# Token loads of the QKV stages: the group behind the next one loaded at a group's 30th product

## The chip, the cores and the metric

The kernel runs on one NeuronCore of one Trainium2 chip. The metric is the time of one execution on the device in microseconds (us); lower is better. Five engines work side by side, each through its own instructions in order: PE (TensorE, matrix products and transposes), DVE (VectorE), ACT (ScalarE), POOL (GpSimd) and SP (SyncE, which here only issues DMAs).

## The reference

One transformer block with adaptive layer norm, for 2 batches of 2048 tokens with 512 features, all in float32: 

```
mod = silu(condition) @ Wada + bada            # six vectors per batch
xm  = layernorm(x, g1, be1) * (1 + sc_a) + sh_a
qkv = xm @ Wqkv                                # 16 heads of 32
x   = x + gt_a * (causal_attention(q, k, v) @ Wproj + bproj)
xm  = layernorm(x, g2, be2) * (1 + sc_m) + sh_m
x   = x + gt_m * (gelu(xm @ W1 + b1) @ W2 + b2)    # 2048 hidden
```

## The kernel before

The two batches are taken one after the other: QKV stage, attention, then the output projection, and at the end the two MLP products for both batches. The projection of batch 0 is interleaved with the preparation of batch 1's QKV stage.

**The QKV stage** (`class Qkv`, `run`). The 2048 tokens are four groups of 512 (`NG` = 4, `MT` = 512). A group's products follow a Strassen-like scheme with seven products in place of eight: token operands are halves of the transposed, normalized tokens `xmT` and differences of these (`token_sum`, tiles `t`), weight operands are blocks of Wqkv and their sums. For each of four chunks of 128 features of q and k (`keys_and_queries`) and then twice for v (`values`) there are seven steps of two 128x256 products by halves; in the trace they are `ps_a`, `ps_b` and `ps_c`. A group so has 42 steps (`STEPS`), and behind each step stands a call of `tick`, which does the side work due at that step number `n`. The seventh step of a chunk is put off behind the first two steps of the next one. With it q or k is split into a high and a low part (`hi`, `lo`; ACT casts, DVE or POOL subtracts) and both are stored to scratch in DRAM through SP (L1031).

**What `tick` does for the next group g + 1.** At n = 3 `load_x(g + 1)` issues four DMAs on SP (L919), one for each 128 tokens, into the four buffers of tile `x`. At n = 10 to 13 DVE takes the statistics of each (`stat`, L218; after the last `rstd` and `shift`, L224 to L226). At n = 15 and 25 ACT scales the tokens in place, two tiles each (L964). At n = 18 and 28 PE transposes them (`ps_xt`, L214) and ACT applies the modulation into `xmT`. At n = 36 to 40 follow the token differences. Group 0 of batch 0 is loaded at the start; for batch 1 groups 0 and 1 are loaded in the projection phase before.

Because there are four buffers of `x` and a group has four tiles, a load must wait until the transposes that read the former group from them are done.

**Other side work in the same ticks.** From group 1 on the first attention scores are already computed between the steps: PE writes a score bank `s` (two banks, pool `ps_s`) and DVE reduces it to row maxima (`mx`; L504 for whole rows, L498 for the causal block). PE cannot write a third score before DVE has reduced the first. In batch 0 the modulation products `ps_mod` take a bank of the same pool, which DVE frees with the sum `mr` (L1425). `Pieces` (its `load` and `add`) loads blocks of W1 (batch 0) and of W2 (batch 1) on SP at fixed tick counts (L1230, L1239), lets POOL form weight sums of them (L1251), and stores these to DRAM for the MLP. The loads fill buffers that are free at that time, named `kst`, `qst` and `vv` in the trace. From n = 10 a group's keys and queries are read back in the layout of the attention (L335, L360).

**What sets the order.** A planner of the tile framework gives each engine one fixed list of instructions. PE's products and many others are kept in the order of the program; the rest is placed by the planner's estimate of when its inputs are ready. SP works through its list in order, and an issue that waits for a buffer, or for data of another engine, holds all issues behind it. SP's list follows the program here.

Of the kernel before, what the change touches and what calls it, by code (L numbers as in the profile page):

```python
# [27 lines left out]
def dit_block_kernel(  # L28
# [46 lines left out]
    NG = T // MT  # L75
# [132 lines left out]
    def act(ins):  # L208

        return tc.keep_in_program_order(ins)  # L210
# [687 lines left out]
    class Qkv:  # L898
# [239 lines left out]
        def run(self, hp, also, early=()):  # L1138

            row = self.row  # L1140
            late = []
            for g in range(NG):
                at = [0]

                def tick():
                    n, at[0] = at[0], at[0] + 1
                    if n >= self.STEPS:
                        return
                    if g + 1 < NG:
                        if n == 3 and g + 1 not in self.xts:  # L1150
                            self.load_x(g + 1)
                        if 10 <= n < 10 + MTT and g + 1 > row.b:
                            self.stats(g + 1, n - 10)
                        if n in (15, 25):
                            self.scaled(g + 1, n // 25)
                        if n in (18, 28):
                            self.norm(g + 1, n // 28)()
                        sums = {36: S1, 38: S2, 40: S3}
                        if n in sums:
                            self.token_sum(g + 1, sums[n])  # L1160
                    elif n == 28:

                        row.rows(0)
                        act(nc.scalar.activation(first, eps, AF.Exp))
                    if g > 0 and n == 2:
                        self.token_sum(g, A22)
                    if n > 9 and self.loads:
                        self.loads.pop(0)()
                    also(g, n)
                    if g > 0 and n >= 7:  # L1170


                        past, of = n - 6, self.STEPS - 7
                        if g == 1:
                            row.score(row.count(cum[0] * past / of, 0))
                        else:
                            past += of * (g - 2)
                            row.score(
                                row.count(
                                    cum[0] + (cum[2] - cum[0]) * past / (2 * of),  # L1180
                                    1 if g == 2 and n < 25 else 2,
                                )
                            )

                for u in range(C + 2):
                    if (g, u) in early:
                        for k, step in enumerate(self.plain(g, u, hp)):
                            step()
                            if k:
                                tick()  # L1190
                        self.token_sum(g, S3)
                        continue
                    if u < C:
                        steps = self.keys_and_queries(g, u, hp)
                    else:
                        steps = self.values(g, u - C)
                    for step in steps[:2] + late + steps[2:6]:
                        step()
                        tick()
                    late = steps[6:]  # L1200
            for step in late:
                step()
            assert not self.loads
# [156 lines left out]
    with pool("wada") as wp, pool("qkv0") as qp, pool("hl0") as hp, pool(  # L1360
# [113 lines left out]
        def also(g, n):  # L1474

            if (g, n) == (0, 7):
                for k in range(4):
                    qkv.weight_sum(nc.gpsimd, k, slice(0, P))
            pieces.tick()
            if g == 0 and n == 22:  # L1480
                load_wada(2, 5)
            elif g in (1, 2) and n == 10:
                qkv.columns = modulation(g + 1)
            elif g in (1, 2) and n == 14:
                qkv.columns()
                if g == 1:
                    load_wada(3, 4)
                else:
                    scale_shift(a2, c2, r_g2, r_be2, 3, 4)
# [837 lines left out]
```

## Time and profile before

| | us |
|---|---|
| median of 3 runs | 2256.44 (2254.54 to 2258.32) |
| profiled execution | 2256.73 |
| its span in the profile | 2255.0 |
| QKV stage of batch 0, groups 0 to 3 | about 28 to 64, 64 to 106, 106 to 155, 155 to 208 |
| QKV stage of batch 1, groups 0 to 3 | about 777 to 816, 816 to 858, 858 to 906, 906 to 956 |

A row of the timeline gives the start in us, the length in us, the engine, the line, the operation, what it writes and reads, and the count of equal instructions merged in it. In brackets stands the time for which the engine was idle before it, and whose end released it. `SPq` is the issue of a DMA, not its transfer. A row of the waits gives the waiting engine and tile, what it waited for, the sum in us, the count and the longest. The granted clock is the share of full speed at which PE was allowed to run.

### The profile page before, as it was taken

To read this page: it belongs to the slowest core of one execution; us is meant where nothing else is said; L and a number is where in the kernel's file an instruction comes from. 1 tells how busy PE (TensorE), PEld (TensorE's weight loads), DVE (VectorE), ACT (ScalarE), POOL (GpSimd) and SP (SyncE) were. 2 spreads that over 40 slices of the span, in tenths; PEclk is the share of its full clock that TensorE was granted. 3 is DMA by queue.
4 is the path that set the end of the run, shared out by engine and by line. 5 is a ranking of instruction groups with operands and counts; after the bars stand their busy time and mean duration, and the time that the engine had idled before them with its cause. 6 is when DMAs were issued, how large, how long until landed. Compare 5 with 4: busy or idle time off the path is not lost.

```text
span 2255.0 us, 33464 instructions
## 1 busy us (share of the span) xinstructions
PE 2211.3 (98%) x12057; PEld 1432.2 (64%) x12057; DVE 1535.7 (68%) x3309; ACT 1004.6 (45%) x2012; POOL 1297.9 (58%) x807
## 2 busy tenths in 40 slices
PE   7999999999999999999999999999999999999998
PEld 6777555555543587855555555345787787688687
DVE  4668766777757666777577767663685586576576
ACT  4434555555564244365656555614322422332410
POOL 4253998998983695199989898444205204304210
PEclk9999999999999999999999999999999999999999
DMA  8877143231324799542324113363353354353433
GB/s 281 251 259 193 43 93 75 62 85 48 106 97 135 252 308 313 142 92 62 85 67 104 44 48 131 109 231 129 109 175 133 123 184 145 108 187 126 158 125 110
DMA packets 160510, 311.57 MB, mean 138 GB/s; under 512 B 16544, under 2 KB 48844, under 8 KB 158552
## 3 DMA queue, kind: packets, MB, share of 16 engines
q1 hardware_dynamic: 155488, 285.53, 41.8%
q0 software_dynamic: 4480, 23.36, 2.7%
q8 instruction: 95, 1.56, 0.3%
q14 instruction: 71, 0.58, 0.1%
q10 hardware_dynamic: 376, 0.55, 0.1%
HBM read 229.95 MB, written 87.29 MB: 141 GB/s over the span
## 4 chain that ended last, share of the span: by engine, by line
PE 89%; DVE 4%; DMA 2%; POOL 2%; ACT 1%; issue 1%; SPq 0%; DVEq 0%; ACTq 0%; POOLq 0%
PE ps_a L206 27%; PE st L206 18%; PE ps_b L206 12%; PE o L206 10%; PE s L206 9%; PE ps_c L206 4%; PE ps_o L206 4%; PE sm L206 3%; DVE junk L498 1%; POOL ee L695 1%; PE ps_xt L214 1%; DMA x<-in_x_dram 1%; ACT e L670 1%; DVE mx L504 1%; PE ps_o L214 1%
## 5 line engine op out<-in xcount | busy, mean ns | idle before, releaser
L670 ACT ACTIVATE e<-st 128x512 f32<-128x512 f32 (+1 forms) x1152 | 575.0, 579 | 362.4 <-PE st L206 321.3
L504 DVE TENSOR_REDUCE mx<-s 128x1 f32<-128x512 f32 x576 | 381.9, 686 | 199.0 <-PE s L206 197.9
L695 POOL TENSOR_TENSOR ee<-ee,e 128x2048 f32<-128x2048 f32 x106 | 485.8, 4583 | 10.3 <-ACT e L670 4.3
L206 PE MATMUL st<-qst,kst 128*128 128x512 f32 (+3 forms) x1280 | 408.7, 386 | 0.0
L206 PE MATMUL s<-kst,qst 128*128 128x512 f32 (+3 forms) x1046 | 382.2, 396 | 8.0 <-DVE mx L498 2.7
L206 PE MATMUL ps_a<-sum,w 128*128 128x256 f32 (+1 forms) x1088 | 328.8, 431 | 0.1
L206 PE MATMUL o<-e,vv 128*32 128x512 f32 (+3 forms) x2560 | 293.2, 537 | 0.3 <-POOL e L682 0.3
L206 PEld LDWEIGHTS st<-qst,kst 128*128 128x128 f32 x1280 | 228.5, 188 | 97.3 <-issue 65.7
L498 DVE CUSTOM_DVE_ANT_0 junk<-s,causal 128x128 bf16<-128x128 f32 (+3 forms) x470 | 220.7, 470 | 61.0 <-PE s L206 46.8
L1795 POOL TENSOR_TENSOR sum<-w 128x256 f32<-128x256 f32 x30 | 21.8, 727 | 397.1 <-DMA w<-w1d 203.1
L206 PEld LDWEIGHTS s<-kst,qst 128*128 128x128 f32 x1046 | 195.4, 189 | 72.4 <-DVE mx L504 15.4
L206 PEld LDWEIGHTS ps_a<-sum,w 128*128 128x128 f32 x1088 | 204.5, 190 | 40.1 <-issue 11.4
L695 POOL TENSOR_TENSOR ee<-e 128x2048 f32<-128x2048 f32 x42 | 192.5, 4583 | 43.5 <-ACT e L670 42.5
L206 PEld LDWEIGHTS <-sel 32*128 32x128 bf16 x1152 | 29.5, 91 | 197.0 <-issue 196.1
L2014 ACT ACTIVATE h<-h,cols 128x512 f32<-128x512 f32 x120 | 76.8, 710 | 136.3 <-DVE h L1716 136.3
L504 DVE TENSOR_REDUCE mx<-st 128x1 f32<-128x512 f32 x192 | 131.0, 682 | 0.5
L682 POOL TENSOR_SCALAR_AFFINE_SELECT e<-e 128x512 f32<-128x512 f32 x128 | 83.3, 669 | 67.2 <-ACT e L670 67.2
L206 PE MATMUL st<-fold,sel 32*128 32x512 bf16 (+1 forms) x1152 | 117.3, 372 | 1.2
L206 PEld LDWEIGHTS o<-e,vv 128*32 128x32 f32 x2560 | 59.1, 108 | 92.3 <-issue 72.8
L1716 DVE TENSOR_TENSOR h<-c,ps_b 128x256 f32<-128x256 f32 x90 | 37.9, 421 | 103.5 <-PE ps_b L206 103.0
L1066 POOL TENSOR_TENSOR lo<-lo,hi 128x512 fp32r<-128x512 f32 x32 | 40.7, 1274 | 114.2 <-ACT hi L1064 109.8
L206 PE MATMUL ps_b<-sum,w 128*128 128x256 f32 (+1 forms) x384 | 95.0, 383 | 0.0
(237 smaller groups left out, 3590.7 us busy)
## 6 DMA issues: line engine op xcount, KB each, us to landing
qst<-q SPq DMA_DIRECT2D x128, 256.0 KB
kst<-k SPq DMA_DIRECT2D x128, 256.0 KB
w<-w1d SPq DMA_DIRECT2D x32, 896.0 KB
w<-w2d SPq DMA_DIRECT2D x28, 1024.0 KB
w<-w2d SPq DMA_DIRECT2D x28, 768.0 KB
q<-hi SPq DMA_DIRECT2D x32, 256.0 KB
q<-lo SPq DMA_DIRECT2D x32, 256.0 KB
k<-hi SPq DMA_DIRECT2D x32, 256.0 KB
```

The lines of the kernel that those rows point to most:

```text
L206: return tc.keep_in_program_order(nc.tensor.matmul(*args, **kw))
L214: return tc.keep_in_program_order(nc.tensor.transpose(dst, src, ident[:n, :n]))
L498: nc.vector.tensor_tensor_reduce(junk[:, :w], x, causal[:, QB - w :], 1.0, MASKED, ALU.add, ALU.max, m,)
L504: self.vector(nc.vector.tensor_reduce(m, x, axis=AX.X, op=ALU.max))
L670: act(nc.scalar.activation(e4[:, h, :w], sts[h][:, :w], AF.Exp))
L682: nc.gpsimd.affine_select(d, d, pattern=[[0, HC], [1, P]], compare_op=ALU.is_ge, fill=0.0, base=0, channel_multiplier=-1,)
L695: act(nc.gpsimd.tensor_tensor(dst, x, y, ALU.add))
L1066: engine.tensor_tensor(lo, d, hi.bitcast(F32), ALU.subtract)
L1716: act(nc.vector.tensor_tensor(dst, x, y, ALU.add))
L1795: act(engine.tensor_tensor(dst, u, v, op))
L2014: nc.scalar.activation(d[j], d[j], AF.Gelu, bias=col(r_b1 + half * HF + fs[j], 1))
```

## The change

In `tick` of a group g a second place for the load is added: at n = 30, two steps behind the last transposes of group g + 1, the tokens of group g + 2 are loaded, if there is such a group. At n = 3 of the next group the load is left out when it has been made (the old condition `g + 1 not in self.xts` does that). This concerns groups 2 and 3 of each batch; group 1 of batch 0 is still loaded at n = 3 of group 0. The order of PE's instructions is the same in both builds. SP's list differs for group 3 of each batch, and DVE's, ACT's and POOL's lists near it in some places, since the planner puts the statistics, the scaling, a cast and a subtraction where it now expects their inputs.

```
                     n, at[0] = at[0], at[0] + 1
                     if n >= self.STEPS:
                         return
+                    if n == 30 and g + 2 < NG:
+                        self.load_x(g + 2)
                     if g + 1 < NG:
                         if n == 3 and g + 1 not in self.xts:
                             self.load_x(g + 1)
                         if 10 <= n < 10 + MTT and g + 1 > row.b:
                             self.stats(g + 1, n - 10)
```

Lines behind the insertion move by two: L1230 of before is L1232 of after, L1251 is L1253.

SP's list near group 3, before and after:

```
batch 0, before:  k store (hi, lo)  kst<-W1 x4  x x4  q store (hi, lo)
batch 0, after:   k store (hi, lo)  x x4  kst<-W1 x4  q store (hi, lo)
batch 1, before:  k store (hi, lo)  vv/kst<-W2 x8  x x4  q store (hi, lo)
batch 1, after:   k store (hi, lo)  x x4  vv/kst<-W2 x8  q store (hi, lo)
```

More of the change, by code (lines that the diff above doesn't have):

```diff
@@ L1148, in tick @@
                         return
+                    if n == 30 and g + 2 < NG:
+                        self.load_x(g + 2)
                     if g + 1 < NG:
```

## The prediction

> **What bounds the kernel now.** I read the page's busy shares and the chain first, then the waits of TensorE (PE) in the eight group windows of the two QKV stages, then the granted clock there, and last the queues of SP, DVE and PE at each token load.
>
> ```profile
> span 2255.0 us, 33464 instructions
> PE 2211.3 (98%) x12057; PEld 1432.2 (64%) x12057; DVE 1535.7 (68%) x3309; ACT 1004.6 (45%) x2012; POOL 1297.9 (58%) x807
> PE 89%; DVE 4%; DMA 2%; POOL 2%; ACT 1%; issue 1%; SPq 0%; DVEq 0%; ACTq 0%; POOLq 0%
> PE ps_xt L214 <- ACT x L964: 1.4, 2, 1.0
> PE s L206 <- DVE mx L498: 2.7, 1, 2.7
> PE ps_xt L214 <- ACT x L964: 1.4, 2, 1.0
> PE ps_xt L214 <- ACT x L964: 4.2, 2, 3.8
> ```
>
> PE is busy 98% of the span and holds 89% of the chain, so time is won only where PE idles or runs at a low clock. The four waits are of the windows 64 to 106, 106 to 155, 816 to 858 and 858 to 906 us: groups 1 and 2 of batch 0, then of batch 1. In each, the tokens of the following group come late: 1.4, 2.7, 1.4 and 4.2 us. Two of them also cost clock:
>
> ```profile
> 74.00:78.00 4.00, 3.07 (x15) 2.40 (x14) 3.67 (x14) 2.64 (x7) 0.00 (x0) 1.00 0.78 225
> 120.00:121.00 1.00, 1.00 (x3) 0.82 (x4) 1.00 (x3) 0.00 (x0) 0.00 (x0) 0.50 1.03 325
> 125.00:126.00 1.00, 1.00 (x4) 0.76 (x4) 0.72 (x3) 0.00 (x0) 0.92 (x2) 0.53 0.36 131
> 877.00:878.00 1.00, 0.62 (x4) 0.62 (x4) 0.00 (x0) 1.00 (x2) 1.00 (x1) 0.50 1.02 166
> 880.00:881.00 1.00, 1.00 (x5) 0.82 (x5) 0.41 (x2) 0.95 (x2) 1.00 (x3) 0.86 1.10 229
> ```
>
> The columns are window and length, busy time of PE, weight load, DVE, ACT and POOL, then the granted clock, DMA share and GB/s. After the 2.7 us gap the clock is 0.50 for six windows of 1 us (first and last shown); after the 3.8 us gap for three, and 0.86 in a fourth. Around the gap of 1.4 us it is 1.00.
>
> **The change, part by part.** It adds and removes no instruction on a computing engine; it moves DMA issues. Four loads could move: group 2 and group 3 of each batch.
>
> *Group 2, both batches: nothing.* In the old order the load stands at the third product of group 1, in the new at the 30th of group 0. Between these places no piece of W1 or W2 is loaded in either batch (pieces are loaded at ticks 26 and 58 of batch 0, 16 and 47 of batch 1; the interval is ticks 30 to 45). SP, which takes its issues in order, has the same order in both builds: the load stands right behind the k store of chunk 3.
>
> ```profile
> 58.57 0.34 SPq L1031 DMA_DIRECT2D k<-lo  x1
> 59.00 1.83 SPq L919 DMA_DIRECT2D x<-in_x_dram  x4
> 816.80 0.32 SPq L1031 DMA_DIRECT2D k<-lo  x1
> 817.21 1.83 SPq L919 DMA_DIRECT2D x<-in_x_dram  x4
> ```
>
> So the two 1.4 us waits stay. The change does in two places of four what its name says.
>
> *Group 3, batch 0: about 5.7 us won.*
>
> ```profile
> 88.92 0.87 PE ps_xt L214 x8
> 107.57 4.91 SPq L1230 DMA_DIRECT2D kst<-in_L_cond_W_dram  x4
> 112.58 1.84 SPq L919 DMA_DIRECT2D x<-in_x_dram  x4
> 110.72 2.02 DVE L504 TENSOR_REDUCE mx<-s 128x1 f32<-128x512 f32 x3 [0.62 <-PE s L206]
> 115.91 0.69 DVE L218 BATCH_NORM_STATS2 stat<-x 128x6 f32<-128x512 f32 x1 [2.07 <-DMA x<-in_x_dram]
> 118.51 0.69 DVE L218 BATCH_NORM_STATS2 stat<-x 128x6 f32<-128x512 f32 x1 [0.90 <-DMA x<-in_x_dram]
> 119.12 0.67 DVE L498 CUSTOM_DVE_ANT_0 junk<-s,causal 128x512 bf16<-128x512 f32 x1
> 113.90 1.92 PE L206 MATMUL ps_mod<-vv,sc 128*32 128x512 f32 x16
> 116.09 1.02 PE L206 MATMUL ps_b<-xmT,wqk 128*128 128x256 f32 x4
> 119.86 0.80 PE L206 MATMUL s<-kst,qst 128*128 128x512 f32 x1 [2.75 <-DVE mx L498]
> 123.55 1.27 POOL L1066 TENSOR_TENSOR lo<-lo,hi 128x512 fp32r<-128x512 f32 x1 [6.78 <-ACT hi L1064]
> 106.00:155.00 49.00, 45.24 (x214) 37.27 (x215) 33.26 (x89) 19.05 (x42) 18.52 (x20) 0.93 0.86 272
> ```
>
> The four x issues move ahead of four piece issues that take 4.91 us, so they start at about 107.6 instead of 112.6. The transposes that read the buffers ended at 89.8, so their wait is over by then. The first tile landed 3.3 us after its issue (112.58 to 115.91) and the third 5.9 us after: now about 110.9 and 113.5. DVE's new order takes the first statistic after two of the three reductions, at 112.0, and the rest after the fourth (it ends at 113.8). None waits for x any longer. The adaptive-norm sum reads `ps_mod`, which ends at 115.8, and L498 reads the score after it: it ends near 117.2, and PE is ready for its next score at 117.1. The 2.75 us gap shrinks to about 0.1. Without it the half clock goes too: six windows at half speed are 3.0 us. That makes 2.75 + 3.0 - 0.1, about 5.7 us, and at most 5.85. What could be late next are the scaled tokens at the transposes; among PE's waits of this window none is for them, and `shift` in the new order follows reductions that PE itself paces, so it moves forward with PE. The lower end is 0, for a load that lands no earlier.
>
> The four piece loads come at least 1.84 us later (the four x issues). They feed sums of POOL, whose results the MLP stage reads over a thousand us later. The cover is POOL's idle time, 6.8 us ahead of its next `lo`; without it a late `lo` would hold the k and q stores. I cost it at nothing.
>
> *Group 3, batch 1: about 3.8 us won.*
>
> ```profile
> 861.25 0.93 SPq L1239 DMA_DIRECT2D vv<-in_L_cond_W_dram  x2
> 865.36 1.84 SPq L919 DMA_DIRECT2D x<-in_x_dram  x4
> 865.31 0.42 DVE L1072 SCALAR_TENSOR_TENSOR lo<-ps_b,lo 128x256 f32<-128x256 f32 x1 [0.22 <-issue]
> 869.84 0.69 DVE L218 BATCH_NORM_STATS2 stat<-x 128x6 f32<-128x512 f32 x1 [0.36 <-DMA x<-in_x_dram]
> 874.98 0.80 DVE L226 SCALAR_TENSOR_TENSOR shift<-mv,rstd 128x4 f32<-128x4 f32 x1
> 871.87 1.03 PE L206 MATMUL ps_b<-xmT,wqk 128*128 128x256 f32 x4
> 876.68 0.33 PE L214 MATMUL ps_xt<-ident,x 128*128 128x128 f32 x1 [3.79 <-ACT x L964]
> 877.38 1.75 PE L214 MATMUL ps_xt<-ident,x 128*128 128x128 f32 x7 [0.38 <-ACT x L964]
> 879.36 1.49 PE L206 MATMUL ps_c<-xmT,wqk 128*128 128x256 f32 x4
> 869.33 1.28 POOL L1251 TENSOR_TENSOR vv<-vv,kst 128x512 f32<-128x512 f32 x1 [0.55 <-DMA kst<-in_L_cond_W_dram]
> 887.73 3.73 POOL L1066 TENSOR_TENSOR lo<-lo,hi 128x512 fp32r<-128x512 f32 x3
> 897.73 0.62 ACT L1064 CAST hi<-lo 128x512 fp32r<-128x512 f32 x1 [2.00 <-DMA q<-hi]
> ```
>
> Here x passes eight piece issues, 861.25 against 865.36, 4.1 us. But DVE is the limit: from 865.3 to 875.8 it runs with idle times of 0.2 to 0.4 us (two of them in the rows). The new order puts the statistics between the score reductions, and two reductions and an L1072 behind `shift`; at about 0.6, 0.6 and 0.4 us each that is 1.6 us, so `shift` ends near 874.2 by counting, and near 873.3 if the waits in between go too. Against that, the statistics hold back two reductions that free score banks: I place waits of PE of 1.2 and 0.6 us at the scores near 868 and 870. PE then reaches the transposes at 874.7 instead of 872.9, and the scaled tokens are there (first transpose 0.9 us after `shift` ends, as before: 876.68 less 875.78). From there to the end of `ps_c` it took 4.2 us (876.68 to 880.85) and should take 2.1 at full clock. So `ps_c` ends at 876.8: about 4.0 us won, 3.8 with another small wait. Upper end: all of the two gaps (4.2) and the clock, 5.7 (0.62 us busy at half speed, two windows whole, one at 0.86: 0.3 + 1.0 + 0.1, about 1.5). Lower end: 0, where the inserted statistics cost PE what the early tokens give; a loss is excluded by nothing but the count above, and belongs to the last rival.
>
> POOL's sums of the delayed pieces start near 871.2 instead of 869.33, and one `lo` now stands in their midst, so the two others, part of the three at 887.73, end about 2 us later than before. The cast that reuses the first one's `hi` buffer comes at 897.7 in the old trace, 893.7 with PE 4 us earlier, and POOL's `lo` ends at 892.1: 1.6 us of cover. Beyond it PE would lose one for one.
>
> *Sum.* 5.7 + 3.8 = 9.5 us. The profiled execution took 2256.73 (span 2255.0), the median of the runs is 2256.44: 2247.2 and 2246.9. I say 2247. The chain through the attention phases behind both stages is PE's own work, so I expect the gain to last.
>
> **Rivals.**
> 1. *The clock falls in batch 1 all the same.* The 3.8 us gap splits into waits of 1.2, 0.6 and perhaps 0.5 us within 6 us. For: a gap of 2.75 us was enough at 119.9. Against: 1.4 us in the window 74 to 78 left it at 1.00, and the batch 1 gaps lie apart with products between. It would cost up to six windows at half speed, 3.0 us: 2250. [...]
> 2. *DVE takes batch 1 back.* The statistics displace reductions one for one. For: DVE is full there. Against: the counted 1.6 us. Only batch 0 gains: 2256.4 - 5.7 = 2250.7.
> 3. *The loads land no earlier.* The DMA share is 0.86 in the window 106 to 155 (row above); the store of a W1 sum and the token load may share the same engines, so that an early issue only queues longer. Against: 3.3 us and 4.5 us from issue to first statistic under the same load. Then the old waits return: 2256.
> 4. *Slower: the statistics block DVE.* They now stand ahead of score reductions, and PE has two score banks. If x lands later than DVE reaches it, DVE waits, the reductions behind it wait, and PE stops. In batch 0 this breaks even when the first tile lands at 115.9, 8.3 us after the issue, and each further us costs PE one. To lose over 4.5 us in all, the tiles of both batches would have to land some 10.6 us after issue: 2261 or more. Nearest rows: 3.3 and 4.5 us.
>
> **How the numbers follow.** A measurement here tells about 0.2%, 4.5 us, from no change. Forecast 0.54 (2247), rival 1 0.17 (2250), rival 2 0.15 (2250.7), rival 3 0.09 (2256), rival 4 0.05 (2261). The range goes from 2244 (both upper ends, 5.85 + 5.7, give 2244.9, and the runs scatter by 2) to 2252 (rival 2 with a scatter of 1) and leaves out rivals 3 and 4, 0.14. Faster is forecast and rivals 1 and 2, 0.86, less 0.04 because rival 2 lies near the 2251.9 bound: 0.82. Same 0.12, slower 0.06.
>
> **What would show it.** Right: SP issues the tokens of group 3 directly behind the k store, near 107.6 and, 5.7 us earlier, near 855.6, with the piece loads behind; no wait of a statistic for x; PE clock 1.00 from 117 to 126; the waits of 1.4 us for group 2 unchanged; the transposes in batch 1 begin about 7.7 us earlier than at 876.68, 5.7 of them batch 0's. Wrong: a DVE statistic waiting for x ahead of a reduction; new waits of PE `s` for DVE `mx` over 2 us in all; a clock of 0.50 near 870; ACT casts waiting for POOL `lo` near 890.

## The result, and the profile after

| | runs | median us | ratio to the kernel before, 95% interval |
|---|---|---|---|
| before | 22 | 2258.05 | 1 |
| changed kernel | 22 | 2252.53 | 0.9974 [0.9968, 0.998] |
| changed kernel, measured again with e9 and e10 | 7 | 2250.54 | 0.9967 [0.9955, 0.9979] |
| changed kernel, measured again with e12 | 8 | 2250.47 | 0.9976 [0.9965, 0.9986] |

The change makes the kernel 0.26% faster, 5.9 us by this ratio (the two medians differ by 5.5). The forecast was 9.5 us and a time of 2247 (2244 to 2252): the direction was right, but only about three fifths of the gain came. The profiled execution took 2252.46 us, span 2250.7.

First the lines that answer to the prediction's first fence, from the page of the changed kernel and from the waits of PE in the windows 64 to 106, 106 to 155, 810 to 852 and 852 to 902 us:

```profile
span 2250.7 us, 33467 instructions
PE 2210.1 (98%) x12057; PEld 1429.4 (64%) x12057; DVE 1537.3 (68%) x3309; ACT 1003.6 (45%) x2012; POOL 1298.3 (58%) x807
PE ps_xt L214 <- ACT x L964: 1.4, 2, 1.0
PE ps_mod L206 <- DVE mx L504: 0.9, 1, 0.9
PE ps_xt L214 <- ACT x L964: 0.9, 2, 0.6
PE s L206 <- DVE mx L504: 0.9, 2, 0.7
PE ps_b L206 <- ACT vv L1130: 0.4, 1, 0.4
```

The waits for group 2 (first and third of them) are still there, as forecast. The two waits for group 3 are gone: 2.7 us in batch 0 has become 0.9 on another bank of the same pool, and 4.2 us in batch 1 has become 0.9 at the scores, 0.3 at the transposes and a new 0.4 on a copy into `vv`. The granted clock around both old gaps, in windows of the changed kernel (columns as in the prediction):

```profile
118.00:130.00 12.00, 11.96 (x66) 9.14 (x59) 10.99 (x27) 5.56 (x12) 6.18 (x8) 1.00 0.93 272
870.00:890.00 20.00, 19.47 (x100) 16.90 (x100) 14.60 (x42) 10.83 (x24) 19.71 (x25) 1.00 0.95 284
```

It is full in both. The same windows of the kernel before had 0.72 (row under e1 and e2 below) and 0.91:

```profile
870.00:890.00 20.00, 15.84 (x73) 13.51 (x72) 13.37 (x39) 9.24 (x19) 19.70 (x25) 0.91 0.95 295
```

So most of the waits and all of the half clock went. To see why less came of it than forecast, I compare the start of the same PE instruction in each profile with its start in the first profile of the kernel before (PE's order is equal in all of them), and take the difference over a stretch. Negative is time won.

| profile | batch 0, 108 to 127 us | batch 1, 866 to 882 us | behind it, 893 to 905 us |
|---|---|---|---|
| before | 0 | 0 | 0 |
| before, second profile (e5) | -2.8 | +1.7 | 0.0 |
| batch 1 alone (e2); batch 0 is old code | -1.9 | -4.3 | +1.1 |
| batch 0 alone (e1); batch 1 is old code | -4.3 | -0.3 | 0.0 |
| changed kernel | -4.6 | -3.9 | +0.6 |
| changed kernel (e11, e13) | -4.2, -4.0 | -4.2, -4.5 | +0.7, +1.3 |
| load one product earlier (e7, e12) | -5.9, -5.9 | -5.2, -5.2 | +1.9, +0.5 |

Two things stand out. The old code of batch 0 is itself 1.9 and 2.8 us faster in other profiles than in the one the forecast was made from. And behind batch 1 something is given back that no profile of the old code shows. The experiments go after both.

### The profile page after: what moved, and what is told of

The parts are those of the page before. It is cut to its first block, busy times and chain, and to the rows that moved or that the text cites. A ratio compares the mean times of both kernels' runs of the same rounds, so it can differ in the third digit from the quotient of the medians.

```text
span 2250.7 us, 33467 instructions
## 1 busy us (share of the span) xinstructions
PE 2210.1 (98%) x12057; PEld 1429.4 (64%) x12057; DVE 1537.3 (68%) x3309; ACT 1003.6 (45%) x2012; POOL 1298.3 (58%) x807
## 4 chain that ended last, share of the span: by engine, by line
PE 88%; DVE 4%; POOL 3%; DMA 2%; ACT 1%; issue 1%; SPq 0%; DVEq 0%; ACTq 0%; POOLq 0%
PE ps_a L206 26%; PE st L206 18%; PE ps_b L206 12%; PE o L206 10%; PE s L206 9%; PE ps_c L206 4%; PE sm L206 3%; PE ps_o L206 3%; DVE junk L498 1%; POOL ee L695 1%; PE ps_xt L214 1%; ACT e L670 1%; DVE mx L504 1%; PE ps_o L214 1%; DVE stat L218 1%
## 5 line engine op out<-in xcount | busy, mean ns | idle before, releaser
L504 DVE TENSOR_REDUCE mx<-s 128x1 f32<-128x512 f32 x576 | 381.6, 686 | 193.4 <-PE s L206 192.4
L504 DVE TENSOR_REDUCE mx<-st 128x1 f32<-128x512 f32 x192 | 131.0, 683 | 0.6
L1066 POOL TENSOR_TENSOR lo<-lo,hi 128x512 fp32r<-128x512 f32 x32 | 40.6, 1274 | 103.9 <-ACT hi L1064 102.0
```

The lines of the kernel that those rows point to most:

```text
L504: self.vector(nc.vector.tensor_reduce(m, x, axis=AX.X, op=ALU.max))
L1066: engine.tensor_tensor(lo, d, hi.bitcast(F32), ALU.subtract)
```

## Experiments

### One batch at a time (e1, e2)

```
-                    if n == 30 and g + 2 < NG:
+                    if n == 30 and g + 2 < NG and row.b == 0:    # e1; row.b == 1 in e2
```

> The new place of the load is kept for batch 0 alone; the program of batch 1 is that of before. By the profile of the changed kernel the steps of PE between group 2's chunk and the next transposes came 4.3 us earlier there (offset of equal PE instructions from +2.2 to -2.1 us). Theory (the two stages win separately, each what its own wait and half clock cost): 4.3 us faster than before, half clock gone near 119 us and still there near 877 us, PE wait of about 4.2 us for the scaled tokens in batch 1 unchanged. Rival (the gain of batch 0 is given back at the head of batch 1, where PE waited 2.4 us instead of 0.7 for an ACT copy behind the layer-norm root): 2.9 us or less, with that wait above 2 us.

> The new place of the load is kept for batch 1 alone. Theory: 3.9 us faster than before (offset of equal PE instructions from -0.6 to -4.5 us in the profile of the changed kernel, 1.6 us of it lost first at the scores near 868 us and more than that won at the transposes), clock 0.50 near 119 us still there, no half clock near 877 us, and the wait of PE for an ACT copy at the head of batch 1 at its old 0.7 us. Rival (the 2.4 us wait there comes from something other than batch 0's gain, such as a transfer that lands late in some executions): it may be seen here too, though nothing ahead of it has changed.

Measured: batch 0 alone 2255.78 us against 2257.29, ratio 0.9994 [0.9985, 1.0003]; batch 1 alone 2253.0, ratio 0.9977 [0.9966, 0.9987]. In us that is 1.4 (from -0.7 to 3.4) and 5.2 (2.9 to 7.7). Batch 1's forecast of 3.8 lies inside its interval; batch 0's 5.7 does not. The miss is mostly in batch 0. The 4.3 us expected of e1, read off a single profile, were missed as well. The rival stated for e1, that a wait of PE for ACT at the head of batch 1 (2.4 us in the first profile of the changed kernel, 0.7 before) takes the gain back, fell too: that wait is 0.7 us in e1, e11 and e13 and 0.9 in e2, so the 2.4 belonged to one execution.

The granted clock says why the old batch 0 has no fixed price. The same window of the kernel before, of e2 and of the second profile of the kernel before (e5), all three with the old code in batch 0:

```profile
118.00:130.00 12.00, 10.14 (x37) 8.49 (x38) 8.21 (x23) 4.18 (x9) 3.99 (x5) 0.72 0.71 223
```

```profile
118.00:130.00 12.00, 10.61 (x47) 9.00 (x48) 10.25 (x25) 5.58 (x11) 4.73 (x6) 0.86 0.68 206
```

```profile
118.00:130.00 12.00, 9.62 (x53) 6.84 (x42) 10.07 (x27) 3.99 (x8) 5.74 (x8) 1.00 0.91 282
```

A mean clock of 0.72 over 12 us is 6.7 us at half speed, 0.86 is 3.4 us, 1.00 is none. Yet the gap was nearly equal in all three: 2.75 us in the first (the prediction's row), and in e2 and e5:

```profile
119.39 0.80 PE L206 MATMUL s<-kst,qst 128*128 128x512 f32 x1 [2.27 <-DVE mx L498]
```

```profile
122.34 0.50 PE L206 MATMUL s<-kst,qst 128*128 128x512 f32 x1 [2.15 <-DVE mx L498]
```

So with gaps of 2.75, 2.27 and 2.15 us in the same code the clock was at half speed for 6.7, 3.4 and 0 us. The length of the gap alone does not set what it costs; what else does, no run here shows.

What half clock costs on average can be read from the timed runs, since each has its mean granted clock on record, to three places. One minus this clock, times the span, is what a run loses to half clock, if PE has work all that time; it is an estimate, and an upper one (the first profiles of both kernels have half clock at their very end, 2252.4 to 2255.0 us before the change and 2248.4 to 2250.7 with it, where PE is busy 0.00 us). The mean over 79 runs of the kernel before is 5.7 us, over 37 of the changed kernel 1.8, over 12 of e1 4.7, over 7 of e2 2.6 and over 11 of e9 (below, the load one product earlier in batch 0 alone) 3.7; these means have standard errors of 0.2 to 0.6 us. So about 4 us of the change's gain are half clock that went. From the runs with one batch changed, some 1 to 2 us of these belong to batch 0, for which 3.0 were forecast, and 2 to 3 us to batch 1, for which 1.5 were.

### The kernel before, once more (e5)

No edit; a second profile of the old code.

> The kernel before, looked at once more. [...] The head of the execution, to 28 us, may differ by up to 2 us. [...]

It took 2265.0 us, above every other timed run of this kernel, so its total is not used. Besides the rows above it shows what else varies between executions of one program. Its PE and ACT in group 1 of batch 1, in which the change does nothing:

```profile
841.24 1.42 PE L206 MATMUL ps_a<-t,wqk 128*128 128x256 f32 x4 [4.32 <-ACT lo L1059]
```

```profile
839.59 0.62 ACT L1064 CAST hi<-lo 128x512 fp32r<-128x512 f32 x1 [5.47 <-DMA k<-hi]
```

One store of `k` was late, ACT's next cast waited 5.5 us for its buffer, and PE 4.3 us for ACT. The first profile of before has nothing there; e8 below has it (3.4 us). The gap in batch 1 was again followed by half clock, for some 6.8 us (clock 0.57 in the window 882 to 890), where the first profile has 3.4.

### The piece loads behind, the tokens where they were (e3)

The kernel before, with the three planned pieces near group 3 moved by one to fourteen ticks, so that SP has the tokens ahead of the pieces without any new load place:

```
-  (room_k, 84, 93)   (room_q, 88, 98)   (room_3, 74, 80)
+  (room_k, 88, 93)   (room_q, 89, 98)   (room_3, 88, 94)
```

> The load stays at the third product as before; instead the W1 piece of tick 84 is loaded at tick 88 (the next one at 89) and the W2 piece of tick 74 at tick 88, its sums from tick 94. SP then has the tokens of group 3 directly behind the k store and the pieces behind them, in both batches, as the changed kernel does by another edit. Theory (all that counts is that the tokens stand ahead of the piece loads on SP, and that DVE's list follows): the same gain as the changed kernel, 5.5 us against before, within 1 us. Rival (the place in the program counts, by the planner's lists of DVE and ACT): less than half of it.

Measured: 2258.23 against 2257.29, ratio 0.9998 [0.9989, 1.0006]: nothing. The expected 5.5 us were missed. But the profile has both gains, -4.6 us in batch 0 and -4.5 in batch 1, so it is SP's order that wins them, whichever edit makes it; and then +7.2 us between 893 and 905. The place, in PE's and in ACT's timeline of e3:

```profile
891.08 1.25 PE L206 MATMUL ps_a<-wv,t 128*128 128x256 f32 x4 [3.00 <-ACT vv L1130]
```

```profile
890.65 0.37 ACT L1130 COPY vv<-ps_a 128x256 f32<-128x256 f32 x1 [9.84 <-POOL lo L1066]
```

L1130 copies the first value products of group 2 into rows of `vv`, and the W2 piece loaded and summed there (`room_3` lies in the same rows) must first be stored to DRAM by POOL. In e3 that store goes out at 887.67:

```profile
887.67 1.63 POOL L1271 DMA_DIRECT2D w2d<-vv  x3
```

The copy starts at 890.65, 3.0 us behind it. (The row of ACT names POOL's `lo`, which ended at 890.59, about the same time; in e7, e10 and e13 ACT's wait ahead of the same copy, 7.19, 5.64 and 6.64 us, ended with the landing of `w2d<-vv`.) PE waits 3.00 and 0.84 us, its next products run slowly (four of them take 2.08 us at 893.18 and 1.91 at 895.48, against 1.03 at 883.69), and 7.2 of the 9.1 us won are gone. The changed kernel has the same chain in small: the piece is loaded 1.8 us later than before (behind the four x issues) while PE arrives earlier. A later profile of the changed kernel, e13, shows it plainest, again in ACT's and in PE's timeline:

```profile
884.22 0.37 ACT L1130 COPY vv<-ps_a 128x256 f32<-128x256 f32 x1 [6.64 <-DMA w2d<-vv]
```

```profile
886.75 1.13 PE L206 MATMUL ps_b<-wv,xmT 128*128 128x256 f32 x4 [0.97 <-ACT vv L1130]
```

The kernel before has no PE wait on L1130 in this window.

### Half of the W2 piece loaded ahead (e8)

The changed kernel, with two of the four quarters of that piece loaded at tick 60 in place of 74:

```
-                self.events.setdefault(load, []).append(lambda: self.load(f, room))
+                self.events.setdefault(early, []).append(lambda: self.load(f, room, (A11, A21)))
+                self.events.setdefault(load, []).append(lambda: self.load(f, room, (A12, A22)))
```

> The changed kernel with the four loads of the last W2 piece that go to the buffer of the values issued at tick 60 instead of 74, ahead of the tokens; the other four stay. In the changed kernel ACT waited 6 us, until 888 us, before its first copy of values of group 2 in batch 1, and PE lost 0.65 us between 893 and 905 us (1.1 us with the new place in batch 1 alone). Theory (that copy waits for the store of the piece that lies in the values' buffer; behind the tokens the piece comes later): ACT's wait ends about 2 us earlier against PE's products there and the 0.65 us go. Rival (POOL's sums are as late whatever the loads do): the wait stays as it is.

Measured: 2252.25 against 2257.57, ratio 0.9978 [0.9969, 0.9987], the same as the change. In the profile the give-back is gone (0.0 us between 893 and 905 in place of 0.6 to 1.3) and PE waits no longer on L1130, so it is shown that the late store held PE. But nothing is won by it: between 866 and 882 e8 wins only 3.3 us, so that from 866 to 905 it comes to the same 3.3 us as the changed kernel (3.2 to 3.4 in its three profiles). The edit also moved the statistics of group 3 to a later place in DVE's list, behind more reductions, and PE waits 1.0 us at the transposes where the changed kernel has 0.3. The edit therefore does not show what the give-back alone is worth.

### The tokens one product earlier (e7, e12, e9)

```
-                    if n == 30 and g + 2 < NG:
+                    if n == 29 and g + 2 < NG:                    # e7, e12
+                    if n == 29 and g + 2 < NG and row.b == 0:     # e9
```

At 29 the four issues stand ahead of the k store of the chunk, at 30 behind it.

> The changed kernel with the load at the 29th product instead of the 30th, one step behind the last transposes. By the program it then stands ahead of the k store of chunk 3, which waits for a cast and a subtraction: on SP the tokens of group 3 move ahead of two more issues in both batches; nothing moves for group 2. Theory (what SP's order still holds back): issue about 1.7 us earlier in batch 0 and about 8 us earlier in batch 1 than in the changed kernel, the 0.95 us wait in batch 0 smaller or gone, the PE waits at the scores of batch 1 (1.5 us) spread or smaller: 1 to 2.5 us faster than the changed kernel. Rival (DVE's and ACT's lists and the store of the W2 piece set the pace there): within 0.5 us of the changed kernel.

> The load one product earlier (29th), in batch 0 alone. Theory: the change's batch 0 part came to about 1.5 us only because its four issues took over 4 us beside the store of a W1 sum, the first tile landed some 6 us after its issue, and a wait of TensorE of about 1 us stayed. With the issue ahead of that store (1.85 us for four, no wait of a statistic for x) batch 0 should be worth 2.75 us and the half clock that goes with it, 0 to 6.8 us of window, so about 4 us on the median: ratio near 0.998, and about 2.5 us faster than the change in batch 0 alone. Rival: where the product stands matters nothing in batch 0, and the gain of the 29th product lies in batch 1: then about 1.5 us, ratio 0.9994 as with batch 0 alone at the 30th product.

> The load at the 29th product, a second time, beside the change on the same chip. Theory: in each profile the issues take 1.85 us and the wait of about 1 us in batch 0 is gone, worth some 1.5 us on PE's path (5.9 against 4.2 to 4.6 us between 108 and 127); the give-back behind batch 1 takes up to 1.2 us of it. So it should be 0.5 to 2 us faster than the change, ratio 0.996 to 0.9967. Rival: the 4 us of the first pair repeat: ratio 0.9957 against 0.9974. Second rival: no difference at all.

> The changed kernel a third time, beside the load at the 29th product. Theory: ratio 0.997 as in the two earlier measurements (0.9974 and 0.9967), about 1 to 2 us behind the 29th product; the profile shows issues of about 4 us for the tokens of batch 0 and a wait of TensorE of about 1 us on L504.

Measured: e7 2248.09 us, ratio 0.9957 [0.9943, 0.997]; e12 2248.1, ratio 0.9965 [0.9953, 0.9976], beside the change in e13, 2250.47, ratio 0.9976 [0.9965, 0.9986]; e9 (batch 0 alone) 2253.77 against 2258.11, ratio 0.9985 [0.9976, 0.9993], 3.4 us where e1 had 1.4. The ratios' intervals of e12 and e13 overlap, and so do those of e9 and e1. All runs together give 2248.09 (11 runs) against 2251.33 (37 runs), a difference of 3.2 us, from about 1.5 to 5.4 by resampling. So the earlier place is faster, by some 2 to 5 us.

The profiles show the mechanism in batch 0 without overlap. SP's issues, then the first statistic on DVE and PE's wait, of the changed kernel:

```profile
109.96 4.42 SPq L919 DMA_DIRECT2D x<-in_x_dram  x4
114.49 2.10 SPq L1232 DMA_DIRECT2D kst<-in_L_cond_W_dram  x4
115.92 0.69 DVE L218 BATCH_NORM_STATS2 stat<-x 128x6 f32<-128x512 f32 x1 [1.57 <-DMA x<-in_x_dram]
117.26 1.92 PE L206 MATMUL ps_mod<-vv,sc 128*32 128x512 f32 x16 [0.95 <-DVE mx L504]
```

And of e7, with the k store that now follows:

```profile
106.56 1.85 SPq L919 DMA_DIRECT2D x<-in_x_dram  x4
108.50 1.65 SPq L1031 DMA_DIRECT2D k<-hi  x1
111.05 3.47 SPq L1232 DMA_DIRECT2D kst<-in_L_cond_W_dram  x4
110.79 0.69 DVE L218 BATCH_NORM_STATS2 stat<-x 128x6 f32<-128x512 f32 x1
```

With the load at 30 the four issues take 4.42 us (3.75 to 4.27 in e1, e6, e11 and e13) and the first tile is there 6.0 us after the first issue; DVE waits 1.57 us for it, the reduction behind it is late, and PE loses 0.95. With the load at 29 they take 1.85 us, the first tile is there when DVE comes to it, and PE has no wait on L504. All four profiles with 29 (e7, e9, e10, e12) win 5.9 us between 108 and 127, all six with the changed batch 0 at 30 (the change, e1, e6, e8, e11, e13) win 4.0 to 4.6. In batch 1 the earlier load wins about 1 us more up to 882 (5.2 in e7 and e12) and gives back 1.9 in e7 and 0.5 in e12. The slow issues belong to a time and not to the tokens: in e7 it is the k store and the pieces behind that are slow (1.65 us for one, 3.47 for four), in the kernel before it was the piece loads (4.91 for four, the prediction's row).

### A W1 store as the cause of the slow issues (e6)

In the profiles of before, of the change and of e7 a POOL store of a W1 sum goes out 1.3 to 1.5 us ahead of the slow issues. The edit delays two pieces so that this store should come later:

```
-  (room_q, 62, 73)   (room_q, 88, 98)
+  (room_q, 62, 84)   (room_q, 94, 100)
```

> The changed kernel with the sums and the store of the second W1 piece moved from tick 73 to 84, so that this 0.9 MB store no longer runs while the tokens of group 3 are issued in batch 0 (the next load into the same buffer goes from tick 88 to 94). Theory (the four token issues took 4.4 us instead of 1.8 and the first tile came 6.0 us after its issue because the store kept the DMA engines busy): issues back to about 2 us, first tile within 3.5 us, the 0.95 us wait of PE in group 3 of batch 0 gone, about 1 us faster than the changed kernel. Rival (the issues are slow by their own sizes): unchanged 4.4 us and 0.95 us.

Measured: 2253.7 against 2257.57, ratio 0.998 [0.9971, 0.9989]. The issues still took 4.27 us, but a store stood in the same place all the same:

```profile
109.11 0.57 POOL L1269 DMA_DIRECT2D w1d<-qst  x1 [0.30 <-POOL qst L1253]
110.44 4.27 SPq L919 DMA_DIRECT2D x<-in_x_dram  x4
```

So the edit did not take the store away and decides nothing. In the changed kernel the DMA share between 110 and 114 was 1.01; whether the store, the k store, or the sum of all makes SP's issues slow is open.

### Both (e10, e11)

The load at 29 with half of the W2 piece early (e10), beside the change as it stands (e11).

> The load at the 29th product, and two of the four quarters of the W2 piece that lies in the values' buffer loaded at tick 60 in place of 74. Theory: what the 29th product gave back at 893 to 905 (1.9 us) came from ScalarE's first copy of the next group's values, which waited for the store of that piece; with half of the loads out of the way the store goes earlier and the 1.9 us stay won: about 2246.5, ratio near 0.995, and no wait of TensorE on the copy into vv over 0.3 us. Rival: the wait has another cause (the sums on GpSimd): then 2248 as before, with the wait still there.

> The changed kernel as it stands, beside the two others on the same chip. Theory: ratio 0.9974 as first measured, about 2252.3, some 4 us behind the load at the 29th product; a second profile should again show issues of about 4 us for the four tiles of batch 0, the first statistic some 6 us after the issue, and a wait of TensorE of about 1 us there. If the long issues were one execution's chance, they take 1.8 us here and the wait is gone.

Measured: e10 2250.68, ratio 0.997 [0.9958, 0.9982]; e11 2250.54, 0.9967. The profile of e10 has the gains (-5.9, -3.9, and +0.3 behind) but its runs spread from 2248.2 to 2255.2, and its median is no better than the change's. Of its seven runs the two slowest (2254.65 and 2255.15) have a granted clock of 0.997 and the others 0.999 to 1.000, so these two lost some 5 us more than the others to half clock; where, no profile shows, since e10's own fell on a run of 2248.3. The expected 2246.5 was missed, and 29 without the early half remains the fastest kernel tried.

### The loads on ACT's queue (e4)

```
-            nc.sync.dma_start(xt, x_rows(self.row.b * NT + g * MTT + t))
+            queue.dma_start(xt, x_rows(self.row.b * NT + g * MTT + t))   # nc.scalar for the load at n == 30
```

> The changed kernel with the loads of the 30th product issued on ACT instead of SP. They no longer stand behind the k and q stores, so the tokens of groups 2 and 3 can be issued soon after the transposes that read their buffers (89.8 us for group 3 of batch 0, where SP came to them at 107.6 to 110). ACT pays 16 issues of about 0.4 us. Theory (what was left of the waits comes from SP's order: 0.95 us of PE in batch 0 group 3, 1.4 and 0.9 us at the transposes of group 2, and up to 1.6 us at the scores of batch 1): 3 to 5 us faster than the changed kernel, 8 to 10 us faster than before, with statistics that nowhere wait for tokens. Rival (ACT's own list is the next limit: an issue that waits for the transposes or for a DMA slot holds PSUM copies behind it): no gain over the changed kernel, with new waits of PE for ACT copies.

Measured: 2269.79, ratio 1.0056 [1.0043, 1.007]: slower by 12.6 us. Batch 0 won its 5.9 us there. It was neither what was expected nor its rival: the waits of PE that grew were for DVE, not for copies of ACT. In batch 1 the issues stood among ACT's other work (those of group 2 two at 789 and 790, the next two at 803 and 804), while the statistics had been placed early in DVE's list:

```profile
796.44 0.69 DVE L218 BATCH_NORM_STATS2 stat<-x 128x6 f32<-128x512 f32 x1 [6.66 <-DMA x<-in_x_dram]
```

```profile
799.92 1.12 PE L214 MATMUL ps_xt<-ident,x 128*128 128x128 f32 x4 [3.31 <-DVE lo L1072]
```

In DVE's list the subtractions into `lo` (L1066, L1072) stand behind that statistic, which waited 6.66 us for x, and PE then waited 3.31 us for L1072. Up to 906 PE waited another 5.0 us for a `lo` and 5.7 us for `vv` of DVE. This is the fourth rival's mechanism, in another kernel.

## Why the prediction was half right

- **Group 2: nothing.** Right. The two waits stay (1.4 and 0.9 us), and SP's order there is the same.
- **Group 3, batch 1: 3.8 us.** Right. The changed kernel won 3.9 us between 866 and 882, by the steps forecast: waits of PE at the scores (forecast 1.2 and 0.6 us, found 0.72 and 0.22), then transposes without the long gap and without half clock. There is some luck in the number: the 1.5 us of half clock were those of a stretch of 3.4 us, where e5 has some 6.8, and by the clock of the timed runs it is 2 to 3 us on average. The rows of the changed kernel:

```profile
868.61 0.50 PE L206 MATMUL s<-kst,qst 128*128 128x512 f32 x1 [0.72 <-DVE mx L504]
870.20 0.50 PE L206 MATMUL s<-kst,qst 128*128 128x512 f32 x1 [0.22 <-DVE mx L504]
873.58 0.27 PE L214 MATMUL ps_xt<-ident,x 128*128 128x128 f32 x1
874.19 0.98 PE L214 MATMUL ps_xt<-ident,x 128*128 128x128 f32 x7 [0.34 <-ACT x L964]
```

- **Group 3, batch 0: 5.7 us. Here the prediction failed, in two terms.** The first is the step "The first tile landed 3.3 us after its issue (112.58 to 115.91) ... now about 110.9 ... None waits for x any longer." It carried the issue time and the latency of one place in SP's queue to another. The row just above it in the prediction showed that issues at the new place took 4.91 us for four. The tile came 6.0 us after its issue, and PE kept a wait of 0.95 us (1.4 and 1.6 in e11 and e13) where 0.1 was forecast: about 1 to 1.5 us lost, and the profiles of e7 and e9 recover it. The statistic that waited 1.57 us for x ahead of a reduction is one of the prediction's own signs of being wrong. The second is "six windows at half speed are 3.0 us". These 3.0 us were that execution's: with nearly the same gap e2 shows half of it and e5 none, and by the clock of the timed runs it is 1 to 2 us on average. The three profiles with the old code stand at 0, -1.9 and -2.8 us, their mean at -1.6, and against that mean the changed kernel's -4.0 to -4.6 are 2.4 to 3.0 us. Timed alone it is 1.4 (-0.7 to 3.4).
- **The delayed pieces: nothing.** A third term that failed, a small one. The prediction saw that the pieces come later, and gave 1.6 us of cover through the `hi` buffer and POOL's `lo`. What runs out first is the buffer `vv`: the store `w2d<-vv` must be done before L1130 writes group 2's values. It costs 0.6 to 1.3 us in the change and 7.2 in e3.
- **Sum.** Worked out from the profiles: 2.4 to 3.0 for batch 0, 3.9 to 4.5 for batch 1, less 0.6 to 1.3, is about 5 to 7 us. Measured 5.9. By the runs' clock about 4 us of it are half clock, where 3.0 + 1.5 were forecast: too much for batch 0 and too little for batch 1, two errors that nearly cancel by luck. So of the 3.6 us that are missing most is time in which PE still waits: some 5 us of waits were to go, and about 2 did. The late first tile and the late store are the two causes found for this.
- **The rivals.** The first (half clock in batch 1 all the same) fell: the clock is 1.00 from 870 to 890 in the changed kernel and in e2, so waits of 0.72 and 0.22 us a product apart did not cost clock. The second (DVE takes batch 1 back) fell by e2, which won 5.2 us with batch 1 alone. The third (no earlier landing) held in part, in batch 0: issued 2.6 us earlier than the first profile of before, the first tile's statistic ran no earlier (115.92 against 115.91); but PE of that execution was itself 2.3 us late by then, so set against PE it came 2.3 us earlier. The fourth was seen only in e4.
- **The range** ended at 2252, half a us below the median, since its cases took the gain of batch 0 whole or not at all: none had the tokens somewhat late, the old gap cheaper than in its one profile, or a cost of the delayed pieces.

## What to carry to other kernels

Before a gap's price is put into a forecast, look whether the clock loss behind it is there in more than one execution: here the gap stayed near its size (2.15 to 2.75 us in three profiles of the same code), while the half clock behind it was 6.8, 3.4 and 0 us. Mean clocks of many runs give an estimate of its average price. A transfer moved in a queue need not keep the issue time and latency of its old place: here four issues that took 1.84 us there, with the first tile in use 3.3 us after the issue, took 4.42 and 6.0 at the new one, and the four issues that stood there before had shown it with 4.91. And when loads are moved behind others, follow each to the buffer it fills and to the next writer of that buffer, not only to the reader of what it brings.

## What the runs showed that was not expected

- Half clock behind the gap of 2.15 to 2.75 us in batch 0 lasted 6.8, 3.4 or 0 us in three profiles of the same code. In the changed kernel a stretch of it came near the start, where the first profile of before has none; this window of the changed kernel has a clock of 0.57, that is 3.4 us at half speed in 4.0:

```profile
19.00:23.00 4.00, 4.00 (x6) 1.67 (x6) 3.86 (x6) 0.80 (x2) 3.84 (x4) 0.57 1.08 366
```

- Before 28 us of the span, ahead of anything the change touches, the profiles stand 0.0 to 3.1 us behind the first profile of before. That alone is over half of the change's effect, so a single pair of profiles can't tell the size, only the place.
- The issue of one DMA on SP took 0.46 us at one place (1.85 for four) and 1.1 us (4.42 for four) or 1.65 (one) at another, 2 us later, in stretches with a DMA share of 0.89 (e7, 108 to 112 us) to 1.01 (the change, 110 to 114). What makes it slow stays open.
